# Layer 1's attention loop: the next tile's scores ahead of the heads' outputs, projection ahead of the queries, statistics behind the sums

## Chip, cores and metric

The kernel runs on one core of one Trainium2 chip. The metric is device time in microseconds (us). Engines are named as in the profile: PE (TensorE), DVE (VectorE), ACT (ScalarE), POOL (GpSimd), SP (SyncE, which only issues DMAs here). Lines such as L956 are lines of the kernel before. Up to L956 the changed kernel has the same numbers.

## What is computed

Two layers on x of shape (2, 2048, 512), each a cross-attention on a context of 128 rows and a feed-forward part, all with a residual. The change touches only layer 1's attention and the first half of its feed-forward part, a gate that picks one of 8 experts:

```python
x = x + attention(layernorm(x), ctx, ctx, mask)      # 16 heads of 32, softmax over 128 keys
h = layernorm(x)
probs = softmax(h @ Wg + bg); p, e = max(probs), argmax(probs) % 8
x = x + relu(h @ We[e] + be[e]) * p
```

## The kernel before

The 4096 rows are 32 tiles of 128 rows. Layer 0 and its feed-forward part take the first 930 us of the trace, layer 1's loop runs from there to about 1432 us, and the experts fill the rest. From the loop on, the four computing engines run their instructions in the order in which the program issues them, each engine its own; nothing is reordered by a scheduler. A tile's buffer that is used again makes the first writer wait for all readers of the old contents, also for those issued later in the text.

The loop has one step n for each tile; two tiles share a block of queries. What a step issues, by helper:

- `scores(n)`: 16 small score matmuls on PE (L892) into the PSUM tile `sc`; then on DVE, for each half of the heads, `s` = masked scores (L900) and the negated maximum `mx` (L905). There is one buffer for each half of `s`, and one `sc`.
- `exponentials(n)`: 16 activations on ACT (L914) in place in `s`; those of the second half also give the row sums.
- `shares(n, half)`: DVE sums the first half (L920), takes a reciprocal `rs` (L922), and POOL multiplies `s` by it (L923).
- `turned(n)`: 16 transposes of `s` on PE (L116), copied back by ACT into the same `s` (L931).
- `mixed(n)`: 16 small matmuls (L941) of that `s` with the values into `po`, the heads' outputs, which ACT copies to `oT` (L946).
- `biased(n-1)` on POOL (L949); `projected(n-1)`: the output projection on PE (L955) and the residual addition on DVE (L956).
- `normed2(n-1)`: statistics of the new x on DVE (L92, L94, L963, L100), a power on POOL (L101), the centred rows `xn2` on DVE (L821). `turned2(n-1)`: 4 PE transposes of them (L116) and an ACT copy (L972).
- `logits(n-2)` on PE (L978), `picked(n-2)` on DVE (L984 to L988), `gated(n-2)` on ACT, DVE and POOL (L996 to L1008).
- `queries(block+1, f)`: two of the next block's four query matmul groups (L872) with an ACT copy each (L875).
- `normed(m)` for a tile m five steps ahead (for m = 4, 5 and 6 somewhat differently): statistics on DVE (L92, L94, L100) and a power on POOL (L101); its later part centres the rows on DVE (L821), splits them (L826) and sends them through a transposing DMA of SP (L829). The turned rows are put together by ACT in pairs at the end of every odd step (`turned1`, L832).
- From step 24 on, pieces of the routing (`routing(True)`); in step 29 the first three expert tiles are centred on DVE (`centered_x`, L104) and the first is transposed on PE and copied by ACT (`turned_x2(0)`, L116 and L1185).

The small PSUM results (`pl`, `pw`, `pq`, `pt`, `po`) share four buffers.

The order within a step is that of the loop's text. In front of the exponentials stand the statistics of tile m, the scores, and either the logits (even steps) or the first query group (odd steps):

```python
firsts = [normed(m) for m in firsts]
scores(n)
late = t == 0 and n > 1
if ahead and not late:
    queries(blk + 1, fs[:1])
if late:
    logits(n - 2)
exponentials(n)
```

and at the step's end `turned(n)`, `turned2(n - 1)`, `mixed(n)`, then `turned1` of odd steps, then the pieces of the routing, and in step 29 `centered_x` and `turned_x2`.

## Time and profile before

| what | value |
|---|---|
| time, median of 3 runs (lowest to highest) | 1597.74 us (1596.93 to 1598.61) |
| the profiled execution's own time | 1599.43 us |
| its span in the trace | 1597.4 us |
| mean granted PE clock | 0.995 |
| PE busy in the span | 1551.3 us (97%) |
| DVE busy | 1192.5 us (75%) |
| ACT busy | 720.4 us (45%) |
| POOL busy | 586.8 us (37%) |

The trace gives each instruction a start and a duration, and says in square brackets how long its engine sat idle before it and which instruction's end released it. Below, a time inside a step is often counted from the start of the step's first `s` (L900); the step that begins at 1104.46 us of the span is step 11.

### The profile page before, as it was taken

The page shows a single profiled execution, that of the slowest core. Times are in us where ns is not written, and L with a number is a line of the kernel's source. Part 1 is how long each engine was busy: PE and PEld are TensorE (multiplying, and loading weights), DVE is VectorE, ACT ScalarE, POOL GpSimd, SP SyncE. Part 2 cuts the span into 40 slices and gives each one's busy share as a digit, 9 for nine tenths or more (in the row PEclk, how much of TensorE's full clock was granted, in tenths as well). Part 3 has the DMA queues.
Part 4 walks back from the last instruction along what each step waited for, and adds up shares of the span by engine and source line. Part 5 has one row for each costly group of instructions (what it writes and reads, how often), then busy time and mean ns, then how long its engine had stood idle before and what let it go on. Part 6 is the DMA issues. An engine that isn't in the chain of part 4 may idle for free. (4 is left out here: it accounts for less than half of the span.)

```text
span 1597.4 us, 26167 instructions
## 1 busy us (share of the span) xinstructions
PE 1551.3 (97%) x9542; PEld 909.1 (57%) x9542; DVE 1192.5 (75%) x2333; ACT 720.4 (45%) x1537; POOL 586.8 (37%) x580
## 2 busy tenths in 40 slices
PE   7999999999999999999999999999999999999997
PEld 5655555555555555544444466666666666654443
DVE  3467777777777886589986678888888888877442
ACT  1222222222222222243335566777777776763442
POOL 2232222222222222110005654555565444544553
PEclk9999999999999999999999999999999999999999
DMA  9511212111111220367768734221311111114553
GB/s 321 188 37 41 47 40 47 40 47 40 51 46 41 59 60 1 117 169 205 179 173 278 271 132 143 48 47 34 55 45 36 41 28 41 41 47 131 162 162 89
DMA packets 180571, 150.90 MB, mean 94 GB/s; under 512 B 97089, under 2 KB 144665, under 8 KB 180444
## 3 DMA queue, kind: packets, MB, share of 16 engines
q1 hardware_dynamic: 170188, 127.25, 28.5%
q0 software_dynamic: 6240, 18.70, 3.8%
q10 hardware_dynamic: 4016, 3.29, 0.9%
q8 instruction: 76, 1.25, 0.3%
q14 instruction: 51, 0.42, 0.1%
HBM read 89.97 MB, written 41.79 MB: 82 GB/s over the span
## 5 line engine op out<-in xcount | busy, mean ns | idle before, releaser
L419 ACT ACTIVATE pr<-sc 128x1024 f32<-128x1024 f32 x64 | 65.6, 1024 | 421.6 <-PE sc L414 421.4
L393 PE MATMUL pq<-xnT,wq 128*128 128x256 f32 x1024 | 254.4, 391 | 0.0
L451 PE MATMUL pw<-wo,att 128*128 128x512 f32 x512 | 230.8, 593 | 0.0
L393 PEld LDWEIGHTS pq<-xnT,wq 128*128 128x128 f32 x1024 | 184.4, 189 | 67.1 <-issue 44.0
L914 ACT ACTIVATE s<-s,mx 128x128 f32<-128x128 f32 x512 | 175.3, 388 | 28.1 <-DVE mx L905 28.1
L923 POOL TENSOR_TENSOR s<-s,rs 128x1024 f32<-128x1024 f32 x64 | 120.9, 1903 | 149.6 <-DVE rs L922 149.1
L403 POOL TENSOR_TENSOR q<-rt,rt 128x256 f32<-128x256 f32 x64 | 46.7, 730 | 339.7 <-DVE rt L402 335.2
L451 PEld LDWEIGHTS pw<-wo,att 128*128 128x128 f32 x512 | 96.9, 190 | 96.4 <-issue 89.9
L441 DVE RECIPROCAL rd<-sc 128x256 f32<-128x256 f32 x64 | 112.4, 1757 | 46.5 <-PE sc L435 46.5
L1195 PE MATMUL pz<-we,x 128*128 x312 | 139.3, 598 | 1.8 <-ACT x L832 1.6
L872 PE MATMUL pq<-xT,wq 128*128 128x256 f32 x512 | 122.6, 382 | 0.0
L978 PE MATMUL pl<-wgate,xnT 128*128 128x512 f32 x256 | 116.7, 599 | 0.0
L955 PE MATMUL pw<-wo,oT 128*128 128x512 f32 x256 | 115.2, 592 | 0.7 <-ACT oT L946 0.7
L872 PEld LDWEIGHTS pq<-xT,wq 128*128 128x128 f32 x512 | 96.0, 190 | 33.1 <-issue 20.3
L398 DVE TENSOR_TENSOR rt<-pq,rope_cos 128x256 f32<-128x256 f32 x64 | 27.0, 422 | 104.2 <-PE pq L393 104.2
L749 ACT ACTIVATE gate<-pg,gsc 128x512 f32<-128x512 f32 x88 | 60.5, 687 | 93.9 <-PE pg L744 84.0
L1195 PEld LDWEIGHTS pz<-we,x 128*128 128x128 f32 x312 | 58.2, 192 | 68.4 <-issue 65.2
L92 DVE BATCH_NORM_STATS2 st<-x 128x6 f32<-128x512 f32 x130 | 89.4, 688 | 6.0 <-DMA x<-in_ctx 3.8
L744 PE MATMUL pu<-xqT,wuT 128*128 128x512 bf16 x352 | 90.3, 379 | 2.6 <-DVE h L752 2.4
L744 PE MATMUL pg<-xqT,wgT 128*128 128x512 bf16 x352 | 90.3, 379 | 0.0
L900 DVE SCALAR_TENSOR_TENSOR s<-sc,keep 128x1024 f32<-128x1024 f32 x64 | 78.1, 1220 | 14.3 <-PE sc L892 9.1
L955 PEld LDWEIGHTS pw<-wo,oT 128*128 128x128 f32 x256 | 48.6, 190 | 55.3 <-issue 53.6
(226 smaller groups left out, 2811.8 us busy)
## 6 DMA issues: line engine op xcount, KB each, us to landing
h_dram<-h SPq DMA_DIRECT2D x88, 256.0 KB
hq<-h_dram SPq DMA_DIRECT2D x31, 704.0 KB
x_dram<-x SPq DMA_DIRECT2D x32, 258.0 KB
x<-in_x SPq DMA_DIRECT2D x32, 256.0 KB
we<-in_L_ffn_We SPq DMA_DIRECT2D x8, 1024.0 KB
xnT<-in_x_turned SPq DMA_DIRECT2D x14, 512.0 KB
along<-stat_dram SPq DMA_DIRECT2D x14, 256.0 KB
w_in<-in_L_ffn_w_gate SPq DMA_DIRECT2D x11, 256.0 KB
```

The costliest lines, as they stand in the source:

```text
L92: nc.vector.bn_stats(out=st, in_=x)
L393: nc.tensor.matmul(pq, wqs[c // 2][:, c % 2, par, g * P : (g + 1) * P], xnTs[k][:, c, :], start=(c == 0), stop=(c == ND - 1))
L441: nc.vector.reciprocal(rd, sc[:, 0, B0:])
L451: nc.tensor.matmul(pw, atts[u][:, f, t * P : (t + 1) * P], wo[:, 2 * g + f, :], start=(g == 0 and f == 0), stop=(g == NG - 1 and f == 1),)
L744: nc.tensor.matmul(dst, w[:, c, i * P : (i + 1) * P], xqTs[blk][:, c, :], start=(c == 0), stop=(c == ND - 1),)
L872: nc.tensor.matmul(pq, wq1[:, c, f * P : (f + 1) * P], xTs[blk][:, c, :], start=(c == 0), stop=(c == ND - 1))
L900: nc.vector.scalar_tensor_tensor(s, sc[:, 2 * half : 2 * half + 2].rearrange("p r c k -> p (r c) k"), -MASKED, keeps[n].unsqueeze(1).to_br ...
L914: nc.scalar.activation(s[:, h, :], s[:, h, :], AF.Exp, bias=mx[:, h : h + 1], **accum)
L923: nc.gpsimd.tensor_tensor(s, s, rs.unsqueeze(2).to_broadcast([P, 8, T]), ALU.mult)
L955: nc.tensor.matmul(pw, os_[n][:, c, :], wo1[:, c, :], start=(c == 0), stop=(c == ND - 1))
L978: nc.tensor.matmul(pl, xn2T[n][:, c, :], wgate[:, c, :], start=(c == 0), stop=(c == ND - 1))
L1195: nc.tensor.matmul(pz, ring[j][:, c, :], we[:, bass.ds(e, 1), c, :], start=(c == 0), stop=(c == ND - 1))
```

## The change

The loop's body is reordered; each computing instruction is still issued, as often and of the same shape.

- `scores(n+1)` is issued at the end of step n, behind `turned(n)`, `turned2(n-1)` and the routing's pieces, and in front of `mixed(n)`. `scores(0)` stands in front of the loop.
- In every step PE gets logits, projection, and then both query groups; ACT gets all exponentials before the copy of the first query group. The projection's matmuls are issued ahead of the exponentials; its residual addition stays behind the shares.
- The statistics of tile m, with POOL's power, move from the start of the step to behind the second `shares`, in front of the residual addition.
- The routing's pieces become a helper, `sort(n)`, called in front of `scores(n+1)`. `centered_x` and `turned_x2(0)` of step 29 stay at the step's end, which is now behind `scores(30)`.

```diff
-        nc.vector.tensor_tensor(xs[n], xs[n], pw, ALU.add)
+        return lambda: nc.vector.tensor_tensor(xs[n], xs[n], pw, ALU.add)
...
+    scores(0)
     for n in range(NT):
...
-        firsts = [m for m in (n + 2 * NB1, n + 2 * NB1 + 1) if m < NT and (m >= TURNED) == (m > n + 2 * NB1)]
-        firsts = [normed(m) for m in firsts]
-        scores(n)
...
-        late = t == 0 and n > 1
-        if ahead and not late:
-            queries(blk + 1, fs[:1])
-        if late:
+        if n > 1:
             logits(n - 2)
+        residual = projected(n - 1) if n > 0 else None
         exponentials(n)
-        if ahead and late:
+        if ahead:
             queries(blk + 1, fs[:1])
...
         shares(n, 0)
         if n > 1:
-            if not late:
-                logits(n - 2)
             picked(n - 2)
         shares(n, 1)
+        firsts = [m for m in (n + 2 * NB1, n + 2 * NB1 + 1) if m < NT and (m >= TURNED) == (m > n + 2 * NB1)]
+        firsts = [normed(m) for m in firsts]
         if n > 0:
-            projected(n - 1)
+            residual()
             normed2(n - 1)()
...
             turned2(n - 1)
+        sort(n)
+
+        if n + 1 < NT:
+            scores(n + 1)
         mixed(n)
...
         if n == NT - NB1 - 1:
             for j in range(3):
                 centered_x(j)
             turned_x2(0)
```

More of the change, by code (lines that the diff above doesn't have):

```diff
@@ L1235, in two_layers, with sort @@
     route = None
+    def sort(n):
+        nonlocal route
+        if n == NTA + 2:
+            route = routing(True)
+        if route:
+            for _ in range({NTA + 2: 4, NTA + 3: 1}.get(n, 2)):
+                if next(route, route) is route:
+                    route = None
+                    for j in range(4):
+                        gathered(j)
+                    break
+    scores(0)
     for n in range(NT):
@@ L1303, in two_layers @@
                 turned1((blk + 2) * NB1 + t)
-        if n == NTA + 2:
-            route = routing(True)
-        if route:
-            for _ in range({NTA + 2: 4, NTA + 3: 1}.get(n, 2)):
-                if next(route, route) is route:
-                    route = None
-                    for j in range(4):
-                        gathered(j)
-                    break
         if n == NT - NB1 - 1:
@@ L1317, in two_layers @@
     biased(NT - 1)
-    projected(NT - 1)
+    projected(NT - 1)()
     normed2(NT - 1)()
```

## Prediction

> **What bounds the kernel now.** I read the page's busy shares first, then the loop's steps one by one in the timeline (start, duration, engine, instruction, idle before it and its releaser), then the timeline of DVE and PE in steps 25 to 30, and last the granted clock in narrow windows. PE is busy 97% of the span, so the loop is PE's unless a chain is nearly as long. Steps 2 to 23 each take 15.32 us from one first `s` (L900) to the next (only step 18 takes 15.43). This is step 11:

> ```profile
> 1103.11 0.67 DVE L92 BATCH_NORM_STATS2 st<-x 128x6 f32<-128x512 f32 x1
> 1104.46 1.22 DVE L900 SCALAR_TENSOR_TENSOR s<-sc,keep 128x1024 f32<-128x1024 f32 x1 [0.28 <-PE sc L892]
> ...
> 1112.64 0.20 DVE L922 RECIPROCAL rs<-sums 128x8 f32<-128x8 f32 x1 [0.24 <-ACT s L914]
> ...
> 1113.22 0.69 DVE L956 TENSOR_TENSOR x<-x,pw 128x512 f32<-128x512 f32 x1 [0.37 <-PE pw L955]
> ...
> 1115.76 0.75 DVE L821 SCALAR_TENSOR_TENSOR xn<-x,mv 128x512 f32<-128x512 f32 x1 [0.66 <-POOL x L101]
> ...
> 1116.63 0.42 PEld L116 LDWEIGHTS pt<-ident,xn 128*128 128x128 f32 x4 [0.29 <-ACT s L931]
> ...
> 1117.22 1.31 PE L941 MATMUL po<-s,v 128*32 128x128 f32 x32
> ...
> 1118.46 1.17 PE L892 MATMUL sc<-kT,qT 32*128 32x128 f32 x32
> ...
> 1119.05 2.55 ACT L832 COPY xT<-xn 128x1024 uint16<-128x1024 uint16 x2
> ...
> 1119.78 1.23 DVE L900 SCALAR_TENSOR_TENSOR s<-sc,keep 128x1024 f32<-128x1024 f32 x1 [0.28 <-PE sc L892]
> ...
> 1122.35 2.79 ACT L914 ACTIVATE s<-s,mx 128x128 f32<-128x128 f32 x9 [0.75 <-DVE mx L905]
> ```

> The reader is to see a second ring almost as long as PE's work: `s`, exponentials, second reciprocal (8.18 us after `s`), residual (8.75), `xn2` (11.30), its transposes (12.20), heads' outputs, scores, next `s`. PE's wait of 0.29 at the transposes is put down to ACT, but `xn2` ends only at 1116.51, 0.12 earlier; step 27, whose residual came sooner, has `xn2` 10.98 and the transposes 11.88 after `s`, the same 0.90 behind. So the ring already stops PE once a step. Its slack is what the residual waits for the projection: 0.45 from where it could start, since step 25 shows 0.12 from reciprocal to residual without a wait (1330.44 to 1330.56). The statistics cost nothing where they stand: they fill DVE's hole while PE does outputs and scores, and `s` waits 0.28 more after them.

> **Part 1: statistics behind the shares.** The three instructions L92, L94, L100 back to back take 1.02:

> ```profile
> 1337.58 0.68 DVE L92 BATCH_NORM_STATS2 st<-x 128x6 f32<-128x512 f32 x1
> 1338.30 0.18 DVE L94 BATCH_NORM_AGGREGATE mv<-st 128x2 f32<-128x6 f32 x1
> 1338.52 0.15 DVE L100 TENSOR_SCALAR ve<-mv 128x1 f32<-128x1 f32 x1
> 1338.60 1.23 DVE L900 SCALAR_TENSOR_TENSOR s<-sc,keep 128x1024 f32<-128x1024 f32 x1
> ```

> Now they queue on DVE between reciprocal and residual, with the residual and the whole of `normed2` behind them. The residual starts at 8.18 + 0.12 + 1.02 = 9.32 instead of 8.75: +0.57. The hole they leave stays empty, because the next `s` waits for PE. On POOL the power of tile m now comes behind the shares (end 10.45, power 0.55, so 11.0) and before that of x, which is wanted at 9.32 + 1.97 = 11.29: no cost, at most 0.29 to spare.

> **Part 2: logits, projection, queries.** PE's work is the same. The projection ends one or two query groups earlier (1.72 each), about 6.9 after `s`, so the residual's wait is gone: that is the 0.45 which Part 1 has used up. The first query copy of odd steps moves behind the exponentials on ACT; it only holds a PSUM buffer until about 8.9, and the next user comes after 10. Nothing.

> **Part 3: scores before outputs.** `s` has one buffer, which the outputs still read, so the next `s` waits for the outputs where it waited for the scores. From the transposes' start to `s` it was 3.12 (12.20 to 15.32). Now: transposes 0.56, scores 1.11 (1103.14 to 1104.25), outputs 1.01 (step 27, 1367.39 to 1368.40; 1.24 in step 11, where they wait for ACT's copies, which the scores now cover), less 0.13 for the two of sixteen matmuls that read only the second half, plus 0.41 from the last matmul to `s`: 2.96. Between -0.16 and +0.1; I take -0.15. An odd step thus grows by 0.57 - 0.15 = **0.42**.

> In even steps ACT is late too. The copy of the outputs started 1.21 before `s`; now it starts about with it. Behind it in odd steps stand the two L832 copies of 2.55, so the next exponentials can start at about 0.48 + 2.55 = 3.03 less 0.1 of overlap, not 2.57: +0.35 (0 to 0.46), all of it on the ring. An even step grows by **0.77**. Steps 2 to 23: 11 x 0.42 + 11 x 0.77 = **13.1**, with the bounds 5 to 19.

> **Part 4: the first steps.** In step 0 tile 4's power stands behind the shares on POOL (they end at 944.06), and DVE, waiting for it, reaches the two `y` additions (L812) that free PSUM for the last two transposes only at about 946.2, not 942.2: scores(1) 1.6 late. Step 1 has two statistics but no longer has two rows of transposes in front of its `s`, and step 2 pays these: -0.5 and about +0.1 beyond Part 3's rate. With a clock drop about **+2** (0 to 4).

> **Part 5: steps 24 to 28.** DVE's routing sets `s` there. Statistics leave the stretch before `s` (1.02) and enter the one before the residual, so steps 24 and 25 come out even; step 26 pays 0.88 + 0.35 with nothing taken away (tile 32 does not exist); step 28 loses its wait for the projection, 0.3 or so. **+0.9** (0 to 2).

> **Part 6: step 29.** `centered_x` and `turned_x2(0)` stood in front of scores(30) and now stand behind:

> ```profile
> 1398.40 2.40 DVE L104 TENSOR_SCALAR x<-x 128x512 f32<-128x512 f32 x3
> 1401.57 1.22 DVE L900 SCALAR_TENSOR_TENSOR s<-sc,keep 128x1024 f32<-128x1024 f32 x1 [0.76 <-ACT x L1185]
> ```

> DVE will do the four instructions of scores(30) first (4.87), then the first centring (0.7), and PE's transposes of it stand in front of logits, projection and expert: PE idles from the outputs' end, 0.3 before `s`, to about 5.55 after it, 5.9. ACT's exponentials are behind the copy L1185 as well, but PE is later than they are. Against it stand 0.9 that step 29 gains (`s` no longer waits for those transposes) and about 0.4 from its other waits: +5.2 so far. The expert stage behind it waits little (PE busy 153 of its 167 us), so all of this lasts. If DVE's order were no limit, 0.

> What a long PE stop does next is in the trace: step 25, where the shares held PE 1.25 and then 0.76 (columns: window, length, busy PE, PEld, DVE, ACT, POOL, granted clock, DMA):

> ```profile
> 1332.00:1333.00 1.00, 0.25 (x2) 0.25 (x3) 0.36 (x3) 0.72 (x2) 1.00 (x2) 1.00 0.00 0
> 1333.00:1334.00 1.00, 1.00 (x8) 0.85 (x6) 0.77 (x2) 0.50 (x1) 0.20 (x1) 0.64 0.00 0
> 1334.00:1335.00 1.00, 1.00 (x6) 0.71 (x4) 0.93 (x4) 0.67 (x2) 0.00 (x0) 0.50 0.00 0
> ```

> The clock is halved for about 3.4 us, so some 1.7 us of work is lost (1.0 to 2.5): step 29 costs **+7** in all. In the loop PE's wait at the transposes grows from 0.3 to about 0.85 (odd) and 1.2 (even); step 27 waited 0.68 and 0.29 within 4 us with no drop, step 25 2.0 with one. I add **+1** for a drop now and then. [...]

> **Sum.** 13.1 + 2 + 0.9 + 7 + 1 = 24.0. The profiled execution took 1599.43 (span 1597.4 and 2.0 around it), so a like one takes 1623.4; it lies 1.7 above the median of the three runs, and the median to expect is 1597.74 + 24 = **1621.7**.

> **Rivals.**
> 1. The clock drops in every even step: about 1.1 more each (in step 25 transposes took 1.02 and outputs 1.74 from start to start, against 0.56 and 1.24), 11 x 1.1 = 12: 1634. For it: the wait there becomes 1.2. Against: step 27. Chance 0.10.
> 2. The ring has slack that I don't see, so that the statistics cost nothing in the loop: 2 + 0.9 + 7 = 9.9, so 1607.6. Against: `xn2` holds PE already. Chance 0.11.
> 3. The stop in step 29 is much smaller (DVE and PE orders leave some way around): 24 - 7 = 17, so 1614.7. Chance 0.08.
> 4. Faster: the earlier projection is worth more than the statistics cost. If `xn2` is there when PE has finished the transposes of `s`, PE's waits go (0.29 and the 0.2 of the outputs, 22 times, 8 to 11 us): with step 29's stop shrunk too, about 1590. It decides from the point where the residual starts before 8.45; the rows give 9.32. Chance 0.04.

> The forecast keeps 0.67. The loop's bounds (5 to 19) with the first steps and step 29 give 1609 to 1631 for it; with rivals 1, 2 and 3 the range is 1608 to 1634. A difference within 0.2% is about what a measurement of this kernel can't tell from no change: slower 0.94, same 0.02, faster 0.04.

> **What would show it.** In the changed profile: the residual about 9.3 after `s` with no wait for `pw`; `xn2`'s transposes at 12.8 with PE idle 0.8 and more before them; `s` released by PE's `po`, not `sc`; steps of 15.7 and 16.1 in turn; exponentials of even steps waiting for ACT's own L832 copies; one PE stop of nearly 6 us before transposes of `x` at step 30, with the clock at half behind it. Steps of 15.0 to 15.3, or no such stop, would prove me wrong.

## The result, and the profile after

The changed kernel takes **1617.1 us** (median of 6 runs, 1612.5 to 1620.8) against 1598.3 us of the kernel before on the same chip (6 runs, 1596.9 to 1599.6): a ratio of 1.0114, 95% interval 1.0103 to 1.0124. So it is slower, as forecast, by 18.8 us where 24 were forecast. Its profiled execution took 1618.03 us (span 1616.3, mean granted clock 0.991), 18.9 us more span than the one of before.

The starts of each step's first `s` cut both spans into the same stretches:

| stretch | before, us | after, us | difference | forecast |
|---|---|---|---|---|
| up to step 0 | 930.17 | 929.60 | -0.6 | none |
| steps 0 and 1 | 36.44 | 40.47 | +4.0 | +2 |
| steps 2 to 23 | 337.07 | 345.27 | +8.2 | +13.1, and +1 for clock drops |
| steps 24 to 28 | 81.98 | 83.32 | +1.3 | +0.9 |
| steps 29 and 30 | 31.71 | 38.77 | +7.1 | +7 |
| step 31 to the end | 180.0 | 178.9 | -1.1 | none |

The timeline of the changed kernel in step 11 and at the start of step 12 (columns: start, duration, engine, instruction, idle before it and its releaser):

```profile
1111.47 1.23 DVE L900 SCALAR_TENSOR_TENSOR s<-sc,keep 128x1024 f32<-128x1024 f32 x1 [0.99 <-issue]
...
1119.66 0.20 DVE L922 RECIPROCAL rs<-sums 128x8 f32<-128x8 f32 x1 [0.24 <-ACT s L914]
1119.78 0.64 DVE L92 BATCH_NORM_STATS2 st<-x 128x6 f32<-128x512 f32 x1
...
1120.75 0.69 DVE L956 TENSOR_TENSOR x<-x,pw 128x512 f32<-128x512 f32 x1
...
1123.30 0.75 DVE L821 SCALAR_TENSOR_TENSOR xn<-x,mv 128x512 f32<-128x512 f32 x1 [0.66 <-POOL x L101]
...
1124.19 0.63 PE L116 MATMUL pt<-ident,xn 128*128 128x128 f32 x4 [0.55 <-DVE xn L821]
...
1124.75 1.17 PE L892 MATMUL sc<-kT,qT 32*128 32x128 f32 x32
...
1125.86 1.08 PE L941 MATMUL po<-s,v 128*32 128x128 f32 x32
...
1127.03 1.23 DVE L900 SCALAR_TENSOR_TENSOR s<-sc,keep 128x1024 f32<-128x1024 f32 x1 [0.99 <-issue]
...
1128.73 1.34 ACT L832 COPY xT<-xn 128x1024 uint16<-128x1024 uint16 x1
...
1129.93 2.73 ACT L914 ACTIVATE s<-s,mx 128x128 f32<-128x128 f32 x9
```

The reader is to see the statistics between reciprocal and residual, the residual 9.28 after the step's `s` (8.76 in the step shown of before) and no longer waiting for `pw`, PE stopped by `xn2` (0.55 on the row of the matmuls and 0.76 on that of their weight loads, PEld, where before shows 0.29), the scores in front of the outputs, and in the even step that begins at 1127.03 the exponentials 2.90 after `s`, without a pause behind ACT's own L832 copies. Odd steps last 15.56 and even ones 15.82. The busy times of these two steps (columns: window, length, busy PE, PEld, DVE, ACT, POOL, granted clock, DMA) show that PE idles in them at full clock:

```profile
1111.47:1127.03 15.56, 15.01 (x117) 10.02 (x118) 13.10 (x28) 10.52 (x35) 9.18 (x9) 1.00 0.22 34
1127.03:1142.86 15.83, 15.02 (x117) 10.04 (x118) 13.10 (x29) 12.88 (x37) 9.17 (x9) 1.00 0.27 52
```

The stop at step 30, on PE, then on DVE, then in the granted clock (same columns as above):

```profile
1412.29 1.08 PE L941 MATMUL po<-s,v 128*32 128x128 f32 x32
1418.92 1.08 PE L116 MATMUL pt<-ident,x 128*128 128x128 f32 x4 [5.56 <-DVE x L104]
1419.80 5.51 PE L978 MATMUL pl<-wgate,xnT 128*128 128x512 f32 x7
```

```profile
1413.46 1.23 DVE L900 SCALAR_TENSOR_TENSOR s<-sc,keep 128x1024 f32<-128x1024 f32 x1 [2.32 <-PE po L941]
1414.72 1.22 DVE L905 TENSOR_REDUCE mx<-s 128x8 f32<-128x1024 f32 x1
1415.85 1.21 DVE L900 SCALAR_TENSOR_TENSOR s<-sc,keep 128x1024 f32<-128x1024 f32 x1
1417.10 1.22 DVE L905 TENSOR_REDUCE mx<-s 128x8 f32<-128x1024 f32 x1
1418.24 1.45 DVE L104 TENSOR_SCALAR x<-x 128x512 f32<-128x512 f32 x3
```

```profile
1416.00:1417.00 1.00, 0.00 (x0) 0.00 (x0) 1.00 (x1) 0.00 (x0) 0.00 (x0) 1.00 0.00 0
1417.00:1418.00 1.00, 0.00 (x0) 0.00 (x0) 0.97 (x2) 0.00 (x0) 0.00 (x0) 0.84 0.00 0
...
1420.00:1421.00 1.00, 1.00 (x3) 0.48 (x2) 0.00 (x0) 0.95 (x3) 0.00 (x0) 0.50 0.00 0
...
1424.00:1425.00 1.00, 1.00 (x3) 0.53 (x2) 0.52 (x2) 1.00 (x7) 0.28 (x1) 0.75 0.00 0
```

DVE works off the four instructions of scores(30) before it centres the first tile; the transposes are next in PE's order, so PE stands 5.56 us, and the clock is at half for 6.8 us, from about 1417.7 to 1424.5.

### The profile page after: what moved, and what is told of

Read it like the earlier page. It is cut to its first block, busy times and chain, and to the rows that moved or that the text cites. A ratio compares the mean times of both kernels' runs of the same rounds, so it can differ in the third digit from the quotient of the medians.

```text
span 1616.3 us, 26211 instructions
## 1 busy us (share of the span) xinstructions
PE 1547.9 (96%) x9542; PEld 907.7 (56%) x9542; DVE 1185.7 (73%) x2333; ACT 720.9 (45%) x1537; POOL 585.8 (36%) x580
## 3 DMA queue, kind: packets, MB, share of 16 engines
q8 instruction: 76, 1.25, 0.3%
## 5 line engine op out<-in xcount | busy, mean ns | idle before, releaser
L914 ACT ACTIVATE s<-s,mx 128x128 f32<-128x128 f32 x512 | 174.5, 389 | 36.1 <-DVE mx L905 36.1
L978 PE MATMUL pl<-wgate,xnT 128*128 128x512 f32 x256 | 120.3, 614 | 0.0
L955 PE MATMUL pw<-wo,oT 128*128 128x512 f32 x256 | 115.3, 593 | 1.4 <-ACT oT L946 1.4
L872 PE MATMUL pq<-xT,wq 128*128 128x256 f32 x512 | 116.3, 379 | 0.0
L900 DVE SCALAR_TENSOR_TENSOR s<-sc,keep 128x1024 f32<-128x1024 f32 x64 | 78.0, 1219 | 39.2 <-issue 30.0
L92 DVE BATCH_NORM_STATS2 st<-x 128x6 f32<-128x512 f32 x130 | 88.5, 680 | 5.7 <-DMA x<-in_ctx 3.4
L955 PEld LDWEIGHTS pw<-wo,oT 128*128 128x128 f32 x256 | 48.5, 190 | 62.4 <-issue 60.0
```

The source lines that it names most:

```text
L92: nc.vector.bn_stats(out=st, in_=x)
L872: nc.tensor.matmul(pq, wq1[:, c, f * P : (f + 1) * P], xTs[blk][:, c, :], start=(c == 0), stop=(c == ND - 1))
L900: nc.vector.scalar_tensor_tensor(s, sc[:, 2 * half : 2 * half + 2].rearrange("p r c k -> p (r c) k"), -MASKED, keeps[n].unsqueeze(1).to_br ...
L914: nc.scalar.activation(s[:, h, :], s[:, h, :], AF.Exp, bias=mx[:, h : h + 1], **accum)
L955: nc.tensor.matmul(pw, os_[n][:, c, :], wo1[:, c, :], start=(c == 0), stop=(c == ND - 1))
L978: nc.tensor.matmul(pl, xn2T[n][:, c, :], wgate[:, c, :], start=(c == 0), stop=(c == ND - 1))
```

## Experiments

**Theory**, that of the prediction: the loop's time is set by the ring through the residual and `xn2`, which already stops PE, so statistics in that ring cost nearly their length and an earlier projection would shorten it. **Rival**: what set the loop before is PE's own line with ACT's copies of the turned `s` (L931) in it, and the residual's ring had slack. The experiments take the three edits of the loop apart (statistics, order of the projection, swap of scores and outputs), and the end of step 29 by itself. All numbers of steps are from the profiled execution, counted from the step's first `s`.

| kernel | time, us (range) | ratio to before, 95% | steps 0, 1 | steps 2 to 23 | step 30 |
|---|---|---|---|---|---|
| before, first chip | 1598.3 (1596.9 to 1599.6) | 1 | 36.4 | 337.1 | 15.8 |
| changed | 1617.1 (1612.5 to 1620.8) | 1.0114 (1.0103 to 1.0124) | 40.5 | 345.3 | 24.0 |
| e1 all but the statistics | 1597.0 (1594.6 to 1600.5) | 0.9979 (0.9968 to 0.9989) | 32.0 | 329.4 | 23.1 |
| e4 all but the swap | 1613.4 (1611.0 to 1615.5) | 1.0083 (1.0060 to 1.0107) | 41.3 | 343.2 | 16.2 |
| e5 statistics alone | 1608.3 (1606.8 to 1610.1) | 1.0052 (1.0032 to 1.0072) | 40.1 | 342.9 | 15.8 |
| e6 order alone | 1597.1 (1595.7 to 1599.5) | 0.9983 (0.9973 to 0.9992) | 33.9 | 337.7 | 15.8 |
| e9 swap alone | 1597.4 (1595.6 to 1600.3) | 0.9986 (0.9974 to 0.9997) | 32.0 | 332.6 | 23.2 |
| e2 changed, step 29 mended | 1614.2 (1612.1 to 1615.4) | 1.0083 (1.0061 to 1.0105) | 38.2 | 345.0 | 16.2 |
| e11 the same, other chip | 1611.0 (1606.8 to 1614.7) | 1.0059 (1.0039 to 1.0078) | 40.4 | 345.4 | 15.2 |
| e10 changed, chip of e11 | 1616.5 (1614.3 to 1620.1) | 1.0105 (1.0080 to 1.0130) | 38.2 | 345.0 | 22.7 |
| e3 e1 and e2 together | 1590.2 (1587.6 to 1591.7) | 0.9930 (0.9908 to 0.9952) | 32.0 | 329.4 | 16.2 |
| e12 the same, chip of e11 | 1586.6 (1583.6 to 1587.6) | 0.9914 (0.9895 to 0.9934) | 32.0 | 329.4 | 15.2 |
| e8 e3, ACT's copies turned round | 1583.4 (1580.8 to 1585.6) | 0.9897 (0.9881 to 0.9914) | 32.0 | 327.5 | 15.2 |
| e7 changed, statistics twice | 1650.8 (1647.9 to 1652.3) | 1.0308 (1.0289 to 1.0328) | 40.8 | 373.2 | 23.8 |

In the last three columns, read from one trace each, half clocks count too. In steps 0 and 1 the clock is at half for 3.4 us before and in e2, e5 and e10, for 6.8 in e7, for 10.2 in the changed kernel, e4 and e11, and in the other rows not at all.

Each row is set against runs of the kernel before on its own chip: 1599.9 us (e1 to e4), 1600.0 (e6 to e9), 1600.9 (e5, e10 to e12).

### e1: all but the statistics

The changed kernel with the statistics back in front of the scores' work on DVE.

```diff
+    def statistics(n):
...
+    coming = statistics(0)
     scores(0)
...
         shares(n, 1)
-        firsts = [m for m in (n + 2 * NB1, n + 2 * NB1 + 1) if m < NT and (m >= TURNED) == (m > n + 2 * NB1)]
-        firsts = [normed(m) for m in firsts]
+        firsts = coming
...
         sort(n)
...
+        nxt = statistics(n + 1)
         if n + 1 < NT:
             scores(n + 1)
...
+        coming = nxt
```

`statistics(n)` holds the two lines that are taken out behind the shares; what it starts is kept in `coming` until the next step uses it.

> The changed kernel with one part undone: the statistics of tile m go back in front of the scores' DVE work (now at the end of the step before). Theory A (the statistics sit in the ring between second reciprocal and residual): the residual starts 8.3 to 8.6 after s instead of 9.27, xn2 at about 11.0, PE no longer waits more than 0.2 at its transposes, steps 2 to 23 take 15.0 on average instead of 15.68, and the time falls by about 15 to 17 us to 1600 (1596 to 1604); the stop of step 30 stays. Theory B (the growth comes from the swap: s waits for the outputs, and ACT's copies come late): steps stay at 15.5 and more, time above 1611.

Measured: 1597.0, and steps of 14.81 and 15.02 in turn. The residual comes at 8.30 (8.54 in even steps), and in an odd step PE does not idle from one `s` to the next:

```profile
1100.00:1114.81 14.81, 14.81 (x118) 10.03 (x117) 13.07 (x29) 11.06 (x35) 9.21 (x9) 1.00 0.26 37
```

The place of the statistics is worth 345.3 - 329.4 = 15.9 us in steps 2 to 23, and 8.5 in steps 0 and 1, some of that by clock drops that e1 does not have there. It is the whole loss of the change, and more: without it, the other two edits shorten the loop well below that of before, and the stop in step 30 eats most of this.

### e6: the order of logits, projection and queries alone

Set against the kernel before:

```diff
-        if late:
+        if n > 1:
             logits(n - 2)
+        residual = projected(n - 1) if n > 0 else None
         exponentials(n)
-        if ahead and late:
+        if ahead:
             queries(blk + 1, fs[:1])
```

Statistics stand in front and scores behind the outputs, as before.

> The kernel before with one part of the change alone: logits, projection, then both query groups in every step (scores behind the outputs, statistics in front of the scores). If the earlier projection is what gains in the runs so far, the residual starts at 8.3 instead of 8.75 after s, PE's wait at xn2's transposes goes, and steps 2 to 23 take 15.0 to 15.1 in odd and even steps alike: 1599 - 6 = 1592 to 1594. If instead the swap is what gains, steps stay at 15.3 and the time at 1598 to 1600.

Measured: 1597.1; my 1592 to 1594 missed. The residual moved to 8.30 as thought, 0.45 earlier, and the step still takes 15.32. The timeline of step 11 of this kernel tells where the 0.45 went:

```profile
1110.52 0.65 DVE L956 TENSOR_TENSOR x<-x,pw 128x512 f32<-128x512 f32 x1
...
1113.12 2.05 ACT L931 COPY s<-pt 128x512 f32<-128x512 f32 x4
...
1114.17 0.60 PE L116 MATMUL pt<-ident,xn 128*128 128x128 f32 x4
...
1114.70 1.58 PE L941 MATMUL po<-s,v 128*32 128x128 f32 x32
...
1115.22 0.79 PEld L941 LDWEIGHTS po<-s,v 128*32 128x32 f32 x26 [0.35 <-ACT s L931]
...
1117.54 1.23 DVE L900 SCALAR_TENSOR_TENSOR s<-sc,keep 128x1024 f32<-128x1024 f32 x1 [0.58 <-PE sc L892]
```

The transposes of `xn2` wait for nothing now, but the outputs behind them stop after a few of their matmuls for ACT's copies of `s`. These end at 1115.17, 12.95 after the step's `s` at 1102.22; in the step shown of before they end at 1117.41, again 12.95 after `s`. In both kernels the scores start 14.00 after `s`. So PE's 0.29 at the transposes of before cost nothing: had `xn2` come sooner, PE would have stood as long in the outputs. This is the rival, and the theory falls on this point. The 3 us that the kernel gains are outside steps 2 to 23: 2.5 in steps 0 and 1, 1.5 in steps 24 to 28. In each of these two stretches the trace of before has a half clock of 3.4 us (at 961.2 and at 1333.3) and that of e6 none, so up to 1.7 us of each may be the clock; the runs don't tell the two apart.

### e9: the swap of scores and outputs alone

Set against the kernel before:

```diff
+        sort(n)
+        nxt = statistics(n + 1)
+        if n + 1 < NT:
+            scores(n + 1)
         mixed(n)
```

The order of logits, queries and projection is that of before.

> The kernel before with the swap alone: scores in front of the outputs (statistics in front of the scores, order of logits, projection and queries as before; centring of step 29 behind the scores). From the rows: transposes to s takes 2.84 instead of 3.12 in odd steps, with ACT's copies 0.3 late in even ones. The residual still waits for the projection (8.65 or so), which sets the ring: odd steps about 15.0 to 15.1, even 15.3; with the stop of step 30 (+8) and 3 us gained in the first steps about 1600 (1596 to 1604). If the swap by itself lengthens the ring (s waiting for the outputs), steps are above 15.4 and the time above 1606.

Measured: 1597.4 with steps of 15.08, odd and even. Step 11:

```profile
1109.17 0.69 DVE L956 TENSOR_TENSOR x<-x,pw 128x512 f32<-128x512 f32 x1 [0.40 <-PE pw L955]
...
1111.32 2.05 ACT L931 COPY s<-pt 128x512 f32<-128x512 f32 x4
...
1112.62 0.63 PE L116 MATMUL pt<-ident,xn 128*128 128x128 f32 x4
...
1113.17 0.98 PEld L892 LDWEIGHTS sc<-kT,qT 32*128 32x128 f32 x32 [0.17 <-issue]
1113.17 1.18 PE L892 MATMUL sc<-kT,qT 32*128 32x128 f32 x32
...
1114.28 0.81 PEld L941 LDWEIGHTS po<-s,v 128*32 128x32 f32 x32
1114.28 1.08 PE L941 MATMUL po<-s,v 128*32 128x128 f32 x32
```

ACT's copies end at 1113.37, under the scores, and the outputs run 1.08 without a stop. With that wait gone the residual's ring does set the time: it waits 0.40 for `pw` and the step is 12.23 to the transposes and 2.85 from there. Swap and order together (e1) take that wait away too, and PE is the bound in odd steps. So the swap is worth 0.24 a step alone and the order nothing alone, but together 0.5 in odd and 0.3 in even steps. In this kernel, too, step 30 takes 23.2 us, which gives back 7.4 of the 8.9 us gained in steps 0 to 23.

### e5: the statistics alone

```diff
-        firsts = [m for m in (n + 2 * NB1, n + 2 * NB1 + 1) if m < NT and (m >= TURNED) == (m > n + 2 * NB1)]
-        firsts = [normed(m) for m in firsts]
         scores(n)
...
         shares(n, 1)
+        firsts = [m for m in (n + 2 * NB1, n + 2 * NB1 + 1) if m < NT and (m >= TURNED) == (m > n + 2 * NB1)]
+        firsts = [normed(m) for m in firsts]
```

> The kernel before with the statistics alone moved behind the second shares; scores, outputs, logits, projection and queries stay where they were. Theory (the residual sets the ring): residual at 8.18 + 0.12 + 1.02 = 9.32 after s instead of 8.75, the rest of the ring unchanged (3.12 from the transposes to s), so steps 2 to 23 of 15.89, +12.5; with some 1 to 2 in the first steps and in steps 24 to 28 about 1614 (1611 to 1618). Rival (the ring has slack for them): steps of 15.3 to 15.4, below 1603. If the outputs lose their wait for ACT's copies as they did with the projection early, steps of about 15.65 and 1609.

Measured: 1608.3, steps of 15.59. The residual comes at 9.27, 0.52 later than before, yet the step grows by 0.27: not by the 0.57 of the theory, nor by nothing, but by nearly what I had written for the case that the outputs lose their wait (0.33). The timeline, PE in step 11:

```profile
1121.29 0.63 PE L116 MATMUL pt<-ident,xn 128*128 128x128 f32 x4 [0.59 <-DVE xn L821]
...
1121.85 1.08 PE L941 MATMUL po<-s,v 128*32 128x128 f32 x32
```

The outputs start 13.27 after `s`, behind ACT's copies, and take 1.08 in place of 1.31. So of the 1.02 us of statistics about 0.5 go into the wait for the projection, another 0.25 into slack that the residual's ring had at the outputs, and only the last 0.27 show.

### e4: all but the swap

```diff
-        if n + 1 < NT:
-            scores(n + 1)
         mixed(n)
...
+        if n + 1 < NT:
+            scores(n + 1)
```

> The changed kernel without the swap: scores behind outputs, turned1 and the expert tiles in every step; statistics behind the shares and the order logits, projection, queries stay. Theory A: the residual stays at 9.3, an odd step takes about 15.83 (0.28 more, since the outputs wait for ACT's copies again), an even one the same (ACT's copies are early again), the stop of step 30 goes: 1617 + 3 - 8 = 1612 (1608 to 1615). Theory B: steps of 15.3, about 1600.

Measured: 1613.4, in the range; the step was 15.59, not as expected, and the same in odd and even steps: that of e5. With the statistics in the ring, the swap hides nothing any more. It makes odd steps 0.03 shorter (15.56) and even ones 0.23 longer (15.82), because ACT's L832 copies start later, so over steps 2 to 23 it costs 2.1 us where it gains 4.5 by itself.

### e2, e10, e11: the end of step 29

The changed kernel with scores(30) behind outputs and centring in step 29 only; e10 is the changed kernel again, beside e11 on one chip.

```diff
-        if n + 1 < NT:
+        if n + 1 < NT and n != NT - NB1 - 1:
             scores(n + 1)
         mixed(n)
...
             turned_x2(0)
+            scores(n + 1)
```

> The changed kernel, but in step 29 alone the scores go behind the outputs, the centring and the transposes of the first expert tile again. Theory A (PE's stop comes of DVE doing the four score instructions in front of the centring): step 30 takes about 15.8 instead of 24, the time falls by 7 to 8 us to about 1609, and the runs scatter less, since the clock no longer drops there. Rival (the stop is the landing of the gathered rows, or the clock): the stop stays, time within 2 us of 1617.

Measured in e2: step 30 fell from 24.0 to 16.2, with no clock drop, but the time fell by 3 us only. Part of that is a half clock of 3.4 us behind the loop (at 1446.8), which the trace of the changed kernel lacks. Another part is step 28: in that execution, and in those of e1, e3 and e4 on the same chip, DVE and ACT both sat still although PE had finished; the timeline of e3:

```profile
1375.89 1.23 DVE L900 SCALAR_TENSOR_TENSOR s<-sc,keep 128x1024 f32<-128x1024 f32 x1 [3.21 <-remote]
```

That is 1.7 us more than the step takes elsewhere. Did it come with the order or with the chip?

> The changed kernel once more, on one chip with the two kernels after it, so that the steps behind step 23 can be compared. 1617 (1613 to 1621); step 28 takes 16.2 if the 1.7 us seen there in four other kernels belonged to their chip or to their order, 17.9 if to this chip.

> The changed kernel with scores(30) behind outputs and centring in step 29 alone, beside the changed kernel on one chip. If the 1.7 us in its step 28 belonged to the chip, step 28 takes 16.2 here and the time is 6 to 8 below the changed kernel's; if it belongs to the kernel, step 28 takes 17.9 again and the time is 3 to 4 below.

Measured: step 28 took 16.21 in e10 and 16.20 in e11, so it came with the chip, or with the one series of runs on it, and not with the order. In e11 PE turns from the outputs to the transposes of the centred tile and then to the scores without a pause:

```profile
1414.14 1.58 PE L941 MATMUL po<-s,v 128*32 128x128 f32 x32
1415.65 0.66 PE L116 MATMUL pt<-ident,x 128*128 128x128 f32 x4
1416.23 1.17 PE L892 MATMUL sc<-kT,qT 32*128 32x128 f32 x32
```

Step 30 is 7.5 us shorter than in e10 and step 29 1.1 longer, so 6.4 in the traces; the medians differ by 5.5 us, just short of the 6 that I expected. What holds DVE and ACT in that one place on one chip is not settled: the releaser is none that the profile shows.

### e3, e12: statistics in front and step 29 mended

Both edits above, e1's and e2's.

> Both of these edits: statistics in front and step 29 as it was; scores ahead of outputs and the order logits, projection, queries stay. Theory A: the gains add, 1590 to 1594, faster than the kernel before by 0.3 to 0.5%; steps 2 to 23 take about 15.0. Theory B: about 1608.

> Statistics in front and step 29 mended, beside the others on one chip. If step 28's 1.7 us belonged to the chip: about 1587 (1584 to 1589), which leaves 3 to 4 for the order of ACT's copies, of which the loop's even steps make 1.9; if to the kernel, 1590 (1588 to 1592) again.

Measured: 1590.2, and 1586.6 on the other chip, where step 28 takes 16.20 instead of 17.89. Both beat the kernel before.

### e8: ACT's copies of the turned rows ahead of the outputs' copy

On top of e3:

```diff
+        later = t == NB1 - 1 and blk + 2 < nblk
+        if later and n > 1:
+            for t in range(NB1):
+                turned1((blk + 2) * NB1 + t)
         mixed(n)
-        if t == NB1 - 1 and blk + 2 < nblk:
+        if later and n == 1:
             for t in range(NB1):
                 turned1((blk + 2) * NB1 + t)
```

> The kernel with the statistics in front and step 29 as it was (1590.2), and ACT's two copies of odd steps from step 3 on issued in front of the outputs' copy instead of behind it. If even steps are longer because these copies come late (exponentials at 2.88 instead of 2.57), even steps fall from 15.02 to 14.82 and the time by 11 x 0.2 = 2.2 to 1588. If the copy of the outputs is what is needed sooner, PE waits in front of the projection and nothing is gained.

In e3 the two L832 copies stand behind the copy of the outputs and hold the exponentials, which follow without a pause (ACT):

```profile
1143.52 0.59 ACT L946 COPY oT<-po 128x512 f32<-128x512 f32 x1 [1.22 <-PE po L941]
...
1144.00 1.35 ACT L832 COPY xT<-xn 128x1024 uint16<-128x1024 uint16 x1
...
1145.21 1.34 ACT L832 COPY xT<-xn 128x1024 uint16<-128x1024 uint16 x1
...
1146.41 2.73 ACT L914 ACTIVATE s<-s,mx 128x128 f32<-128x128 f32 x9
```

In e8 they fill ACT's idle time, and the exponentials wait for DVE again:

```profile
1108.19 2.60 ACT L832 COPY xT<-xn 128x1024 uint16<-128x1024 uint16 x2
...
1110.62 0.61 ACT L946 COPY oT<-po 128x512 f32<-128x512 f32 x1
...
1112.15 2.78 ACT L914 ACTIVATE s<-s,mx 128x128 f32<-128x128 f32 x9 [0.92 <-DVE mx L905]
```

Measured: 1583.4; odd and even steps take 14.82, which makes 1.9 us over steps 2 to 23. That is the even steps' lateness, which the prediction had priced at 0.35 a step (here 0.2, in the changed kernel 0.26), by itself. My 1588 was reckoned from e3 and its chip; against e12, on a third chip, the gain is 3.3 us, of which 1.4 lies outside these steps and is not explained. It is the fastest version tried, 1.0% below the kernel before (0.9881 to 0.9914).

### e7: the statistics twice

```diff
+        again = list(firsts)
         firsts = [normed(m) for m in firsts]
+        for m in again:
+            mv = variance(xs[m])
+            ve = small.tile([P, 1], F32, name="ve")
+            nc.vector.tensor_scalar(ve, mv[:, 1:2], EPS, None, ALU.add)
```

> The changed kernel with the three statistics instructions of tile m issued twice (the second result is used by nobody), both behind the shares. Theory A: the ring takes up each added microsecond, 0.97 for a second set: steps 2 to 23 go from 15.56 and 15.82 to about 16.5 and 16.8, the time to 1617 + 24 = 1641 (1636 to 1646). If the statistics cost only what the projection's wait no longer hides, there is no slack left and nothing changes that. PE then waits 1.8 to 2.0 at the transposes in each step: if a wait of that length halves the clock, steps take 17.5 and more and the time goes beyond 1655.

Measured: 1650.8, between the two cases. Most steps grow by what DVE adds, 15.56 to 16.56 and 15.82 to 16.8: with no slack left, statistics show in full. But steps 6, 8, 12 and 18 take 18.1 to 18.7, with a half clock of 3.4 us in each. In step 6 the transposes of `xn2` had waited 1.82 us (PE):

```profile
1051.27 0.63 PE L116 MATMUL pt<-ident,xn 128*128 128x128 f32 x4 [1.82 <-DVE xn L821]
```

In this trace the half clocks go with how long PE is busy in the 3.41 us before them. Those of the loop start at 963.67, 1052.42, 1086.55, 1154.82, 1257.22 and 1376.68, which is 26, 10, 20, 30 and 35 times 3.413 us from one to the next. Cut into windows of that length on this grid, the trace shows (columns as above):

```profile
997.80:1001.22 3.42, 1.88 (x17) 1.63 (x16) 2.66 (x7) 2.53 (x5) 1.06 (x3) 1.00 0.00 0
1014.87:1018.28 3.41, 1.62 (x16) 1.40 (x13) 2.65 (x7) 2.05 (x4) 0.83 (x2) 1.00 0.00 0
1049.00:1052.42 3.42, 1.60 (x29) 1.22 (x30) 2.62 (x12) 1.77 (x4) 0.55 (x1) 1.00 0.02 5
1052.42:1055.83 3.41, 3.41 (x57) 2.60 (x50) 1.14 (x4) 0.65 (x2) 3.38 (x4) 0.50 0.49 110
1151.40:1154.82 3.42, 1.38 (x12) 1.03 (x11) 2.66 (x7) 2.01 (x4) 0.70 (x2) 1.00 0.02 5
```

The windows that end at 1001.22 and 1018.28, with PE busy 1.88 and 1.62 us, are followed by full clock, those that end at 1052.42 and 1154.82, with 1.60 and 1.38, by half. The four half clocks of steps 3 to 23 follow windows of 1.38 to 1.60; of the other windows there, one has 1.59 and the rest are busier. In this trace the edge is thus at about 1.6 of 3.41 us. In step 6 the whole wait of 1.82 falls into one window, that with 1.60. Of the ten even steps from 4 to 22, which wait 1.5 to 2.0, four have a half clock, which makes each 1.3 to 1.9 us longer, and of the odd ones, which wait 1.3 to 1.55, none.

So what the prediction's rival 1 feared happens here in four steps, and in the changed kernel in none: with waits of 0.55 and 0.81 the least busy window of its steps 3 to 23 has 2.53 us of PE's work (1233.35 to 1236.76), and none of these steps has a half clock.

## Why the prediction was right, and where it was not

**What bounds the kernel: the step that failed.** The prediction read PE's 0.29 at the transposes of `xn2` as the ring of the residual stopping PE, with no slack but the wait for `pw`. e6 shows that this stop was free: ACT's copies of the turned `s` end 12.95 after `s` and the scores behind the outputs can't start before 14.0. Two paths of almost one length met at the outputs, and the prediction followed the one that it saw wait first. It had read the outputs' wait for ACT's copies as well (1.24 against 1.01), but credited its end to the swap and not to the later `xn2`. Its rival 2 (slack that I don't see) was right by 0.25 of the 0.57, and its rival 4 (an earlier `xn2` is worth 8 to 11 us) needs the swap as well: e1 has it, 7.7 us in steps 2 to 23.

**Part 1** (+0.57): the residual came at 9.28, so +0.52.

**Part 3, the swap** (-0.15): from the transposes to `s` it is 2.84, not 2.97, so -0.28. The terms: transposes 0.56 and scores 1.11 as worked out, but `s` starts 1.17 after the outputs do, where 1.01 - 0.13 + 0.41 = 1.29 was put. The sum of 2.96 was near, its name is wrong: e5 gets 0.25 of the 0.28 with no swap at all, from the late transposes alone. Odd steps thus grow by 0.24, not 0.42.

**Part 3, even steps** (+0.35 more): +0.26. Steps 2 to 23: 11 x 0.24 + 11 x 0.50 = 8.1, and 8.2 measured, for 13.1.

**Part 4** (+2): +4.0 in the profiled execution, +1.7 in that of e10. The difference is the clock: at half for 3.4 us (946.6 to 950.0) and again for 6.8 (963.7 to 970.5) in the one, once for 3.4 in the other. The kernel before has one of 3.4 as well (961.2), so +1.7 is the change at an equal clock.

**Part 5** (+0.9): +1.3, and +0.15 in e10, again with and without a half clock (1346.0 to 1349.4); before has one there too (1333.3 to 1336.7).

**Part 6** (+7): -1.1 in step 29 and +8.2 in step 30, together +7.1; in e10 it is +5.8. The stop (5.56 for 5.9) and its cause came as written, and e11 takes it away. That the size agrees is in part luck: the terms as written, 5.9 - 0.9 - 0.4, make 4.6 and not 5.2, so 6.3 with the clock, and the half clock lasted 6.8 us in this execution, twice what was put, and 3.4 in e10.

**Drops in the loop** (+1): none in steps 3 to 23. **Rest**: 0.6 and 1.1 us less outside the loop, no more than what other executions differ by there (the loop starts at 928.2 to 932.6 us over all kernels, though nothing ahead of it was edited).

The sign was right for the right reason, statistics on the ring and a stop in step 30. The size was 5 too high, and that it was no worse owes something to chance. In steps 2 to 23 the forecast was 5.9 too high: 2.9 from the transposes to `s`, which is the slack, 1.1 at the residual, 1.0 at ACT's copies, and 1 for half clocks that did not come. The first steps took 2.0 more than put, by the half clocks named under Part 4, and the other stretches together 1.2 less.

## What to carry to other kernels

A wait that is printed in front of an instruction is worth only what the next instruction on that engine would not wait instead (here PE's 0.29 at the transposes, which e6 takes away, while its step stays at 15.32): before pricing a path, look up when the other inputs of the instruction behind it are ready. Edits that remove two waits in a row can be worth little one by one and more together (here 0.24 us a step and nothing alone, 0.5 in odd steps together), and a third edit that fills the ring again (here 1.02 us of statistics) takes the gain of both. When work that others wait for is moved past a long stage, look at each special case at the end of the loop: the end of step 29 cost here 7.1 us, nearly as much as steps 2 to 23 together (8.2).

## What was not expected of the hardware

```profile
1376.71:1380.13 3.42, 2.66 (x20) 2.13 (x20) 2.42 (x12) 2.70 (x7) 1.98 (x2) 1.00 0.00 0
```

- In step 28 DVE and ACT resumed 1.7 us late on one chip, in four kernels of four, and in none of the other ten traces. The cause stays open.
